# A two-layer graph network on one core: the edge check split over two engines, the mixing weights folded ahead of the branch, the MLP's start no longer tied to the degrees, bias additions and padding rows written elsewhere in the order

## The chip, the cores and the metric

The kernel runs on one core of one Trainium2 chip. The time is that of one execution on the device, in microseconds (us). The engines of the core are named as in the profile: PE (TensorE, matrix products; PEld is its weight load), DVE (VectorE), ACT (ScalarE), POOL (GpSimd) and SP (SyncE, which here only issues transfers). Each engine works through its own queue in order; semaphores hold an instruction until its inputs are there. Transfers are issued on SP's and ACT's queues, the indirect ones (gathers by index) on POOL's.

## The reference

The graph has 3125 nodes with 256 features and 50000 edges, sorted by their target. `xn` is the layer norm of `x`.

```python
# layer 0
xn = layernorm(x)
h = xn @ W                                   # gnn: messages
deg = segment_sum(1, dst);  dis = where(deg > 0, rsqrt(max(deg, 1)), 0)
gnn = segment_sum(h[src] * (dis[src] * dis[dst])[:, None], dst)
hm = layernorm(xn, ln1_g, ln1_b) @ Wx + bx   # mix: 8 heads of 32
q = softmax(heads(hm) @ Wq, -1);  k = softmax(heads(hm) @ Wk, over the nodes)
fx = merge(q @ (k.T @ (heads(hm) @ Wv))) @ Wo + bo + xn
mix = gelu(layernorm(fx, ln2_g, ln2_b) @ W1 + b1) @ W2 + b2 + fx
x = x + gnn + mix
# soft experts: all 8 experts for every node, weighted
z = layernorm(x);  w = softmax(z @ Wr + br)
x = x + sum_e w[:, e] * (relu(bn2(relu(bn1(z @ W1[e])) @ W2[e])) @ Wo[e] + bo[e])
# layer 1: attention over the edges, a hyperbolic mixer, a shared MLP
# and the two best of 8 experts for every node (routed by index)
```

## The kernel before

Nodes are tiled as T = 25 tiles of P = 125 nodes, in seven chunks of four tiles (the last has one). `X` holds the running sum, `XN` the current normalised input, both in SBUF for the whole run.

**Prologue.** The edge list may be used in blocks only if the edges of each tile lie within 128 × LE = 2176 entries of the sorted list. To check this the kernel loads `dst` and counts, for each of the 25 tiles, how many targets lie below its bound (L309 to L311, 25 passes of ACT over 125 × 400 values with a sum). A product with ones adds the partitions (L317), a chain of small DVE operations makes `lidx` (rows of the edge list to fetch) and `nbi` (the number of misfits), and a branch on `nbi` (L2142) selects the usual path, `in_order`, which this input takes. Beside it DVE normalises all 25 tiles (L346 to L372). The prologue's order on each engine is found by the framework's scheduler.

**Layer 0** (class `Layer0`). The body is a set of generators, and `Flow` writes their order out by hand: each `yield Op(engine, cost, after, take, give, lag)` states a planned cost, marks of other steps that must be planned before, and buffers taken and given back. `Flow.run` always emits next the step that can start first by the plan, and on a tie the stream of lower urgency. The plan fixes the order of instructions on each engine; in the run an instruction waits only for the data and buffers that it really uses.

- `first` (L663) loads the weights of the stage and folds the norm's gain into `wx` and `xb` (four groups of small products and DVE operations, L692 to L720).
- `listing` (L786) fetches the edge lists by 25 indirect gathers, turns the target columns (`dl`) by PE and writes them to DRAM (`dlT`). For each tile it then reads them back broadcast to all partitions (`db`, 544 KB each, two buffers), and a Sign pass on ACT with a sum (L823) counts; a product and a Newton root give `dis`.
- `mix_in` transposes a chunk (`tr_mix`) and projects it (`xm`, L855); `messages` makes `hU` (L868, scaled by ACT); `q_softmax`, `k_softmax` and `mix_out` form the attention; `kw` is the last product of the key side, and `at` (L971) gives `fx`, one mark for each tile.
- `table` (L979) scales `hU` by `dis` and splits it into three bf16 parts by turns of ACT and DVE; SP writes them to the table `hs3`.
- `bias` (L1043) adds `mix_b2` to `X` on POOL, one operation of 125 × 1024 for each chunk.
- `after_mixing` (L769) waits for all `fx`, all `hU` and `dis`, closes the pool of the mixing stage and loads the experts' weights (24 transfers of 256 KB); the mark `mixed` follows.
- `mlp_stream` (L561) is the MLP of a chunk: statistics and scaling on DVE, transposes, two activations into `hT`, eight products `hp` with a gelu each, and products `dn`. Its transposes wait for `mixed` by the plan.
- `edges` (L1004) needs `mixed` and all tables: for each tile, in three groups of up to six edge columns, POOL gathers message rows (`msg`, two buffers), DVE builds a 0/1 matrix `S` (three buffers), SP writes it out for layer 1 (`hot`), and PE sums.
- `after_mlp` waits for the MLPs and the tables; `soft_work` (L749) then writes the padding rows of the table `xs` (8,224 KB by one transfer; layer 1 uses `xs` for routing) and, behind it on the same queue, loads `f_bo`, `f_wr`, `w3` and `wc`.
- `soft_in`, `expert` and `soft_out` are the experts of a chunk, its second norm (mark `ch["d"]`) and the projections to `qtab` and `kvtab`; `ball` writes `ztab`. A chunk starts when its tiles have their edge sums.

**Layer 1** (from L1373) follows in a plan of its own.

The urgencies, in `mixing_flow` and `mlp_flow`, are −1 for `listing` and `k_softmax`, 0 for `mix_in` and `mix_out`, 1 to 3 for the others of the stage, 4 for `edges`, 5 for the MLP, 10 and more for the experts.

Of the kernel before, what the change touches and what calls it, by code (L numbers as in the profile page):

```python
# [7 lines left out]
F32 = mybir.dt.float32  # L8
# [3 lines left out]
OP = mybir.AluOpType  # L12
# [138 lines left out]
def kernel(ctx: ExitStack, tc: tile.TileContext, a: dict, out: bass.AP):  # L151
# [41 lines left out]
    check = ExitStack()  # L193
    edge = check.enter_context(tc.tile_pool(name="check", bufs=1))
# [4 lines left out]
    nc.scalar.dma_start(out=nxt, in_=a["dst"][1 : E + 1].rearrange("(p j) -> p j", j=EP))  # L199

# [27 lines left out]

    away = keep.tile([128, 128], F32, name="away")
# [4 lines left out]
    before = keep.tile([128, 128], F32, name="before")  # L234
    nc.vector.tensor_scalar(before, away, 0.0, None, op0=OP.is_lt)
# [18 lines left out]
    zeros = keep.tile([128, W], F32, name="zeros")  # L254
    nc.vector.memset(zeros, 0.0)
# [30 lines left out]
    def turned(dst_, src_, nt, name, nk=2, g=None, b=None):  # L286

        for k in range(nk):
# [6 lines left out]
            else:  # L295
# [6 lines left out]
    bound = edge.tile([P, T], F32, name="bound")  # L302
    nc.gpsimd.iota(bound, pattern=[[P, T]], base=P, channel_multiplier=0,
                   allow_small_or_imprecise_dtypes=True)
    nc.vector.tensor_scalar(bound, bound, -0.5, None, op0=OP.add)
# [3 lines left out]
    for b in range(T):  # L309
        nc.scalar.activation(sign, dstf, AF.Sign, bias=bound[:, b : b + 1], scale=-1.0,  # L310
                             accum_out=cnt[:, b : b + 1])  # L311
    nc.vector.tensor_tensor(below, dst, nxt, OP.is_gt)
    nc.vector.tensor_reduce(cnt[:, T:], below, AX.X, OP.add)
    with ExitStack() as st:
        psum(st, nm=1)
        pc = nm_tile([128, T + 1], "counts")
        nc.tensor.matmul(pc, allone[:P, :], cnt, start=True, stop=True)  # L317
        ends = edge.tile([128, T + 1], F32, name="ends")
        nc.vector.tensor_scalar(ends[:, :T], pc[:, :T], 0.5, E / 2.0, op0=OP.mult, op1=OP.add)
        nc.vector.tensor_copy(ends[:, T:], pc[:, T:])  # L320
# [21 lines left out]


# [3 lines left out]
    mva = check.enter_context(tc.tile_pool(name="norm", bufs=1)).tile([P, T, 2], F32, name="mva")  # L347
    ra = small.tile([P, T], F32, tag="ra", name="ra", bufs=1)
    rb = small.tile([P, T], F32, tag="rb", name="rb", bufs=1)
    for c0, c1 in ((0, 2), (2, 4), (4, 7)):  # L350
        for c in range(c0, c1):
            t0, nt = CHUNKS[c]
            for j in range(nt):
                st_ = small.tile([P, 6], F32, tag="st", name=f"st_a{c}_{j}")
                nc.vector.bn_stats(st_, X[c][:, j, :])
                nc.vector.bn_aggr(mva[:, t0 + j, :], st_)
        ts = slice(CHUNKS[c0][0], CHUNKS[c1 - 1][0] + CHUNKS[c1 - 1][1])
        var = mva[:, ts, 1]
        nc.vector.tensor_scalar(rb[:, ts], var, 1e-5, None, op0=OP.add)
        nc.scalar.activation(ra[:, ts], rb[:, ts], AF.Sqrt)  # L360
        nc.vector.reciprocal(ra[:, ts], ra[:, ts])
        nc.vector.reciprocal(rb[:, ts], rb[:, ts])
        nc.vector.tensor_tensor(rb[:, ts], rb[:, ts], var, OP.mult)
        nc.vector.tensor_scalar(rb[:, ts], rb[:, ts], 1e-5, None, op0=OP.add)
        nc.scalar.activation(irs[:, ts], rb[:, ts], AF.Sqrt)
        nc.vector.reciprocal(rb[:, ts], irs[:, ts])
        nc.vector.tensor_tensor(ra[:, ts], ra[:, ts], rb[:, ts], OP.mult)
        for c in range(c0, c1):
            t0, nt = CHUNKS[c]
            for j in range(nt):  # L370
                nc.vector.tensor_scalar(XN[c][:, j, :], X[c][:, j, :], mva[:, t0 + j, 0:1],
                                        ra[:, t0 + j : t0 + j + 1], op0=OP.subtract, op1=OP.mult)  # L372
# [15 lines left out]
    nc.sync.dma_start(out=qtab[N : N + 1, :], in_=zeros[:1, :C])  # L388


    def degrees():
        with tc.tile_pool(name="deg", bufs=1) as dp:
# [20 lines left out]
            HJ = EP // 2  # L413
            hot_b = dp.tile([P, P, HJ], BF16, name="hot_b")
            hot_a = dp.tile([P, T, HJ], BF16, name="hot_a")
            for g in range(2):
# [18 lines left out]
    def slow_load(pool):  # L435
# [3 lines left out]
        for name, pad in (("src", 0), ("dst", N)):  # L439
# [8 lines left out]
            )  # L448
        e["dstf"] = pool.tile([128, EJ], F32, name="all_dstf", bufs=1)
# [23 lines left out]
    def slow_edges0(e):  # L473
# [4 lines left out]
        with tc.tile_pool(name="e0", bufs=3) as ep:  # L478
            G = 4
            for g in range(EJ // G):  # L480
# [5 lines left out]
                nc.vector.tensor_tensor(sb, S, before[:, None, :].to_broadcast([128, G, 128]), OP.mult)  # L486
# [74 lines left out]
    def mlp_stream(c, inputs, name, pool_of, w1, w2, g, b, b1, done, start):  # L561
# [20 lines left out]
        mk = yield Op("PE", 0.48 * nt, [m, start], take=["mm", "mm", "mlp"])  # L582
# [49 lines left out]
    NQ = NH * 4  # L632
    WX = C + 1 + 2 * NQ
    Q0, K0 = C + 1, C + 1 + NQ

    class Layer0:
# [26 lines left out]
        def first(self):  # L663
# [3 lines left out]
            self.hUt = lp.tile([P, T, C], F32, name="hU")  # L667
            mp = self.mix = self.open("mix", side="right")
            self.wx = mp.tile([128, 2, WX], F32, name="wx")
            wxr = self.wxr = mp.tile([128, 2, C], F32, name="wxr")  # L670
            nc.sync.dma_start(out=wxr, in_=a["Wx"].rearrange("(k p) d -> p k d", p=128))
            wxT = mp.tile([128, 2, C], F32, name="wxT")
            nc.sync.dma_start(out=wxT, in_=a["WxT"].rearrange("(k p) d -> p k d", p=128))
            wqk = mp.tile([128, 2, 2 * NQ], F32, name="wqk")
            nc.sync.dma_start(out=wqk, in_=a["Wqk"].rearrange("(k p) d -> p k d", p=128))
# [1568 lines left out]
```

## Time and profile before

| what | value |
| --- | --- |
| median of 3 runs | 2831.29 us (2821.73 to 2831.99) |
| profiled execution, time | 2825.43 us |
| its span in the trace | 2823.6 us |
| mean granted clock of PE in it | 0.953 |
| PE busy | 2502.8 us, 89% |
| branch entered (first issue behind it) | 41.11 us |
| `dis` ready | 195.6 us |
| table written, first message gather | about 260 us |
| MLP's last product, then the padding's issue | about 424 us, 428.59 us |
| last message gather | about 858 us |
| experts of layer 0 end | about 1275 us |

The page gives the busy time of each engine, then the span in forty slices of 70.6 us, each digit the busy share in tenths. A row of the timeline reads: start, length, engine, line, operation, output and inputs, how many were merged, and in brackets the idle time before it and what ended it. Two things help: an idle engine that is not the bound costs nothing, and the row of a transfer on SP shows its issue, so that a long one means a queue that was full.

### The profile page before, as it was taken

What the parts mean: (1) busy time and instruction counts of PE and PEld (TensorE: products, weight loads), DVE (VectorE), ACT (ScalarE), POOL (GpSimd) and SP (SyncE); (2) the same over time, 40 slices, a digit from 0 to 9 for tenths busy, and PEclk for the clock granted to TensorE, in tenths of its full rate; (3) what the DMA queues carried; (4) which work ended last, traced back from release to release, by engine and by line L of the source; (5) the groups of instructions that cost most, each with busy time, mean ns of one, the idle gap of its engine ahead of it and who ended that gap; (6) DMA issues with size and microseconds to landing.
All of it is one profiled execution on the core that took longest, in us unless ns stands there. A gap on an engine that the chain in (4) does not pass through costs nothing. (4 is left out here: it accounts for less than half of the span.)

```text
span 2823.6 us, 32362 instructions
## 1 busy us (share of the span) xinstructions
PE 2502.8 (89%) x11409; PEld 1822.1 (65%) x11409; DVE 1404.1 (50%) x3527; ACT 963.8 (34%) x2020; POOL 1158.5 (41%) x1145
## 2 busy tenths in 40 slices
PE   3769994999999989996778988888888999999998
PEld 2436773666665645564556756666666668888885
DVE  5476112253453243445889888988886301111113
ACT  3465111222233333444334444444442222222221
POOL 3202774777771000002766655655522632222220
PEclk9869996999999999998889999999999999999999
DMA  4263668666661011106766665666630245555545
GB/s 109 97 201 108 174 177 242 176 190 197 177 199 50 1 33 55 41 25 223 226 199 197 213 196 168 193 188 207 193 110 1 64 162 195 196 196 188 196 147 141
DMA packets 187211, 427.02 MB, mean 151 GB/s; under 512 B 31644, under 2 KB 116765, under 8 KB 178846
## 3 DMA queue, kind: packets, MB, share of 16 engines
q0 software_dynamic: 80688, 281.78, 32.7%
q1 hardware_dynamic: 104650, 141.38, 16.0%
q10 hardware_dynamic: 1700, 1.69, 0.2%
q8 instruction: 92, 1.51, 0.2%
q14 instruction: 81, 0.66, 0.1%
HBM read 358.95 MB, written 65.74 MB: 150 GB/s over the span
## 5 line engine op out<-in xcount | busy, mean ns | idle before, releaser
L1431 POOL DMA_INDIRECT kvg<-kvtab,el x425 | 461.2, 1085 | 312.8 <-issue 105.8
L1010 POOL DMA_INDIRECT msg<-hs,el x425 | 423.2, 996 | 337.7 <-DMA hot<-S 175.2
L1119 ACT ACTIVATE fh<-fp,bnh,bns 128x500 f32<-128x500 f32 (+1 forms) x224 | 160.5, 723 | 357.8 <-PE fp L1115 357.6
L1508 PE MATMUL es<-kvg,S 128*125 128x264 f32 x850 | 226.4, 419 | 50.0 <-DVE kvg L1500 49.6
L1986 PE MATMUL rh<-xrT,rw 128*128 128x256 f32 x1024 | 237.2, 380 | 0.0
L1974 ACT ACTIVATE rhid<-rh,rw 128x256 f32<-128x256 f32 x256 | 121.5, 475 | 336.8 <-PE rh L1986 336.8
L2001 PE MATMUL ry<-rw,rhid 128*128 128x256 f32 x1024 | 231.5, 379 | 0.0
L1508 PEld LDWEIGHTS es<-kvg,S 128*125 128x125 f32 x850 | 166.9, 202 | 98.6 <-DVE kvg L1500 66.1
L1130 DVE SCALAR_TENSOR_TENSOR x<-fy,f_w,x 125x256 f32<-125x256 f32 x200 | 96.3, 482 | 264.7 <-PE fy L1127 263.8
L1033 PEld LDWEIGHTS <-S 128*125 128x125 bf16 x1275 | 155.1, 140 | 91.1 <-issue 80.0
L2001 PEld LDWEIGHTS ry<-rw,rhid 128*128 128x128 f32 x1024 | 194.6, 190 | 26.9 <-issue 0.5
L1127 PE MATMUL fy<-f_Wo,fh 128*125 128x256 f32 x800 | 206.6, 383 | 5.1 <-DVE x L1130 4.9
L1467 PE MATMUL qe<-q,ST 125*128 125x256 bf16 x1275 | 171.7, 276 | 43.5 <-DVE kvg L1471 37.5
L1986 PEld LDWEIGHTS rh<-xrT,rw 128*128 128x128 f32 x1024 | 189.4, 190 | 28.5 <-ACT rhid L1974 5.0
L2008 DVE TENSOR_TENSOR yr<-ry,rw 128x256 f32<-128x256 f32 x64 | 27.2, 425 | 357.5 <-PE ry L2001 357.5
L1033 PE MATMUL es<-msg,S 128*125 128x256 bf16 x1275 | 184.3, 278 | 22.2 <-DMA msg<-hs,el 20.5
L1115 PE MATMUL fp<-fh,f_W 128*128 128x500 f32 (+1 forms) x448 | 187.2, 546 | 0.3 <-ACT fh L1119 0.3
L1115 PE MATMUL fp<-xT_f,f_W 128*128 128x500 f32 (+1 forms) x448 | 185.2, 540 | 0.0
L1243 POOL TENSOR_TENSOR xn<-xn,row_bp 125x1024 f32<-125x1024 f32 (+1 forms) x7 | 13.8, 1978 | 416.9 <-PE tr_q L554 209.4
L1127 PEld LDWEIGHTS fy<-f_Wo,fh 128*125 128x125 f32 x800 | 143.4, 189 | 62.3 <-issue 37.8
L1467 PEld LDWEIGHTS <-ST 125*128 125x128 bf16 x1275 | 125.3, 99 | 79.2 <-issue 46.6
L1471 DVE TENSOR_TENSOR kvg<-qe,kvg 128x512 f32<-128x512 f32 (+1 forms) x225 | 142.8, 651 | 28.9 <-PE qe L1467 18.7
(420 smaller groups left out, 4235.0 us busy)
## 6 DMA issues: line engine op xcount, KB each, us to landing
db<-dlT SPq DMA_DIRECT2D x25, 544.0 KB
ST<-dlT SPq DMA_DIRECT2D x25, 544.0 KB
hot<-S SPq DMA_DIRECT2D x50, 187.5 KB
Sb<-hot SPq DMA_DIRECT2D x50, 187.5 KB
ztab<-z SPq DMA_DIRECT2D x18, 500.0 KB
z<-ztab SPq DMA_DIRECT2D x12, 750.0 KB
xs<-pad SPq DMA_DIRECT2D x1, 8224.0 KB
xr<-xs SPq DMA_DIRECT2D x32, 257.0 KB
```

Source lines behind the costliest of these rows:

```text
L1010: nc.gpsimd.indirect_dma_start(out=msg[:, i, :], out_offset=None, in_=hs3_rows, in_offset=bass.IndirectOffsetOnAxis(ap=el[:, b, g0 + i : g ...
L1033: nc.tensor.matmul(blk["po"], S[:, i, :], msg[:, i, r * C : (r + 1) * C], start=(g0 + i == 0 and r == 0), stop=(g0 + i == LE - 1 and r == 2))
L1115: nc.tensor.matmul(ps[q][:, :n], self.ws[e][i][:, k, q * 128 : (q + 1) * 128], h[:, k, :n], start=(k == 0), stop=(k == 1))
L1119: nc.scalar.activation(nxt[:, q, :n], ps[q][:, :n], AF.Relu, bias=self.sh[i][:, 2 * e + q : 2 * e + q + 1], scale=self.sc[i][:, 2 * e + q ...
L1127: nc.tensor.matmul(po, nxt[:, k, j * P : (j + 1) * P], self.ws[e][2][:, k, :], start=(k == 0), stop=(k == 1))
L1431: nc.gpsimd.indirect_dma_start(out=kvg[:, i, : 2 * C], out_offset=None, in_=kvtab, in_offset=bass.IndirectOffsetOnAxis(ap=el[:, b, g0 + i ...
L1467: nc.tensor.matmul(pq[i0][:, i, :], ST[:P, g0 + i0 + i, :], blk["q3"][:, r, :], start=(r == 0), stop=(r == 2))
L1471: nc.vector.tensor_tensor(kvg[:, i0 : i0 + k, :C], pq[i0][:, :k, :], kvg[:, i0 : i0 + k, :C], OP.mult)
L1508: nc.tensor.matmul(blk["pa"], S[:, i, :], kvg[:, i, C:], start=(g0 + i == 0), stop=(g0 + i == LE - 1))
L1974: nc.scalar.activation(hid[-1][:, q % 2, :], ps, AF.Gelu, bias=w1[:, 8 * C + q : 8 * C + q + 1])
L1986: nc.tensor.matmul(ps, w1[:, k * 4 * C + h * 128 : k * 4 * C + (h + 1) * 128], xrT[:, k, :], start=(k == 0), stop=(k == 1))
L2001: nc.tensor.matmul(po, hid[k // 2][:, k % 2, r * 128 : (r + 1) * 128], w2[:, k * C : (k + 1) * C], start=(k == 0), stop=(k == 7))
```

## The change

1. The edge check: the first 12 bounds are counted on ACT as before, the other 13 by DVE (compare and sum); the bounds are made at the very start. The prologue is now written in a fixed order instead of one found by the scheduler.
2. The loads of `Wx`, its transpose, `Wqk` and the biases, and the folding into `wx` and `xb`, stand in the prologue. Their loads are on ACT's queue, and the products that read them stand partly ahead of the counting product. The tiles live in the pool that stays open; layer 1 reuses their memory for `bd` and `b_res`.
3. Only chunks 0 and 1 are normalised in the prologue; the others are streams of the plan (`normal`), half of the scaling on ACT.
4. `listing` is split into streams (`turned_lists`, `degree`, `degrees`). The degrees' transfers are planned behind the 17th projection.
5. `after_mixing` does not wait for `dis`; the MLP does not wait for `mixed`, and its first two chunks have urgency −1. 21 of the 24 expert weights are loaded in `after_mixing`, three in `soft_work`.
6. `table` works on two tiles at a time, scales on ACT, and uses the `db` buffers; `XT` has five buffers.
7. `bias` is planned behind `kw`; the padding rows are written behind chunk 1's `ch["d"]`.

```diff
     check = ExitStack()
+    check.enter_context(tc.manual_schedule(engines=ENGINES))
...
+    bound = edge.tile([P, T], F32, name="bound")
+    nc.gpsimd.iota(bound, pattern=[[P, T]], base=P, channel_multiplier=0, ...)
+    nc.vector.tensor_scalar(bound, bound, -0.5, None, op0=OP.add)
...
+    nc.scalar.dma_start(out=wxr, in_=a["Wx"].rearrange("(k p) d -> p k d", p=128))
+    nc.scalar.dma_start(out=wxT, in_=a["WxT"].rearrange("(k p) d -> p k d", p=128))
+    nc.scalar.dma_start(out=wqk, in_=a["Wqk"].rearrange("(k p) d -> p k d", p=128))
+    nc.scalar.dma_start(out=bxt, in_=a["bxT"])
+    bx = row(edge, "bx", 128)
...
-    for b in range(T):
+    TA = 12
+    for b in range(TA):
         nc.scalar.activation(sign, dstf, AF.Sign, bias=bound[:, b : b + 1], scale=-1.0,
                              accum_out=cnt[:, b : b + 1])
+    for b in range(TA, T):
+        nc.vector.tensor_scalar(below, dstf, bound[:, b : b + 1], None, op0=OP.is_lt, op1=OP.add,
+                                accum_out=cnt[:, b : b + 1])
     nc.vector.tensor_tensor(below, dst, nxt, OP.is_gt)
     nc.vector.tensor_reduce(cnt[:, T:], below, AX.X, OP.add)
+    for k in range(2):
+        nc.vector.tensor_scalar(wx[:, k, :C], wxr[:, k, :], col("ln1_g", k), None, op0=OP.mult)
+    pb = nm_tile([128, C], "bxm")
...
+    pc = nm_tile([128, T + 1], "counts")
+    nc.tensor.matmul(pc, allone[:P, :], cnt, start=True, stop=True)
...
+    for _ in normal(0, 2, None):
+        pass
     check.close()
...
-    def mlp_stream(c, inputs, name, pool_of, w1, w2, g, b, b1, done, start):
+    def mlp_stream(c, inputs, name, pool_of, w1, w2, g, b, b1, done, start=None):
...
-        mk = yield Op("PE", 0.48 * nt, [m, start], take=["mm", "mm", "mlp"])
+        mk = yield Op("PE", 0.48 * nt, [m] + ([start] if start else []), take=["mm", "mm", "mlp"])
...
         def soft_work(self):
             fp = self.ffn = self.open("ffn")
-            pad = fp.tile([128, C + 1], F32, name="pad")
...
+            self.expert_weights(fp, NE - 1)
+
+        def padding(self, ch):
+            yield Op("POOL", 1.0, [ch["d"]])
+            pad = self.ffn.tile([128, C + 1], F32, name="pad")
+            nc.gpsimd.memset(pad[:, :C], 0.0)
+            nc.gpsimd.tensor_scalar(pad[:, C:], part, float(2 * N), None, op0=OP.add)
+            yield Op("SP", 0.2)
+            nc.sync.dma_start(out=xs.rearrange("(q p) d -> p q d", p=128), ...)
 
         def after_mixing(self):
-            m = yield Op("SP", 2.5, self.fx + self.hu + [self.dis_])
+            m = yield Op("SP", 2.5, self.fx + self.hu)
             self.close("mix")
-            self.soft_weights()
             if self.lists:
                 self.e0 = self.open("e0", side="right")
-            self.mlp_work()
+            self.soft_weights()
             self.mixed.set(m)
...
+        def degree(self, b):
+            m = yield Op("SP", 3.3, [self.rows_[b // 7], self.xm[16]], take=["db"], lag=1.5)
+            db = self.low.tile([128, 128 * LE], BF16, tag="db", name=f"db_{b}", bufs=2)
+            nc.sync.dma_start(out=db, ...)
+            m = yield Op("ACT", 2.25, [m], give=["db"])
+            nc.scalar.activation(db, db, AF.Sign, bias=half, accum_out=self.cnt[:, b : b + 1])
+            self.counted[b].set(m)
...
         def table(self, c):
-                m = yield Op("DVE", 0.4, [self.dis_, self.hu[t]])
-                nc.vector.tensor_scalar(h, h, dis[:, t : t + 1], None, op0=OP.mult)
+                    m = yield Op("ACT", 0.42, [self.dis_, self.hu[t]])
+                    nc.scalar.activation(h, h, AF.Copy, scale=dis[:, t : t + 1])
...
+                m = yield Op("ACT", 0.4 * k, [m], take=["db"])
+                db = self.low.tile([128, 128 * LE], BF16, tag="db", name=f"h3_{t}", bufs=2)
+                h3 = db[:P, : 6 * C].rearrange("p (t i d) -> p t i d", t=2, i=3)
...
         def bias(self, c):
-            yield Op("POOL", 2.0)
+            yield Op("POOL", 2.4, [self.bias_at])
...
         def mixing_flow(self, flow):
+            flow.add(0, normal(2, 4, self.normal))
+            flow.add(0, normal(4, 7, self.normal))
...
         def mlp_flow(self, flow):
-                flow.add(5, mlp_stream(c, self.fx, "m", lambda: self.work, self.w1, self.w2,
-                                       "ln2_g", "ln2_b", "mix_b1", self.mlp_[c], self.mixed))
+                flow.add(5 if c > 1 else -1, mlp_stream(c, self.fx, "m", lambda: self.work, self.w1, self.w2,
+                                       "ln2_g", "ln2_b", "mix_b1", self.mlp_[c]))
...
         def soft_flow(self, flow):
+                if c == 1:
+                    flow.add(10, self.padding(ch))
```

## The prediction

> **What bounds the kernel now.** I read the busy shares first, then the forty slices, then busy time by stretch, and only then the timeline and the waits of the stretches where TensorE (PE) falls short. First the page:
>
> ```profile
> PE 2502.8 (89%) x11409; PEld 1822.1 (65%) x11409; DVE 1404.1 (50%) x3527; ACT 963.8 (34%) x2020; POOL 1158.5 (41%) x1145
> ...
> PE   3769994999999989996778988888888999999998
> ...
> PEclk9869996999999999998889999999999999999999
> ```
>
> PE is busy 89% of the span: PE work is the bound, and time can be won only where PE idles or runs at a low granted clock. In the part that the change touches (slices 0 to 17) the weak slices are 0 to 2 (up to 212 us) and slice 6 (424 to 494 us). The same by stretch (columns: length, busy time and count of PE, weight loads, DVE, ACT, POOL, then granted clock, DMA share, GB/s):
>
> ```profile
> 0.00:41.30 41.30, 0.63 (x2) 0.50 (x2) 26.35 (x129) 20.85 (x58) 1.14 (x12) 1.00 0.42 90
> 41.30:54.40 13.10, 9.60 (x40) 8.82 (x40) 2.31 (x10) 2.31 (x4) 9.53 (x10) 1.00 0.90 275
> ...
> 73.00:89.00 16.00, 2.83 (x16) 2.03 (x14) 16.00 (x10) 0.00 (x0) 14.95 (x8) 0.66 0.01 2
> ...
> 149.50:206.00 56.50, 37.97 (x96) 22.03 (x96) 45.42 (x176) 33.75 (x49) 0.00 (x0) 0.59 0.65 205
> 206.00:262.00 56.00, 55.86 (x195) 36.31 (x196) 46.10 (x168) 36.76 (x89) 0.00 (x0) 0.95 0.32 96
> ...
> 428.00:472.00 44.00, 9.09 (x40) 6.82 (x40) 4.17 (x17) 2.34 (x3) 11.07 (x13) 0.54 1.05 288
> ...
> 858.00:1275.00 417.00, 406.53 (x1405) 242.88 (x1404) 161.68 (x497) 149.53 (x274) 18.75 (x9) 0.98 0.10 30
> ```
>
> Four holes: the prologue (41 us without PE); 73 to 89 (13 us idle); 149.5 to 206 (38 us busy at a clock of 0.59, so 22 us of full-speed work: 34 us lost); 428 to 472 (35 us idle). From 206 to 1275 PE is otherwise full, so what is saved in the holes shifts everything behind them. What ends each hole (timeline, start and length):
>
> ```profile
> 40.29 0.15 DVE L339 CAST nbi<-nbad 128x1 int32<-128x1 f32 x1
> ...
> 41.34 3.57 PE L843 MATMUL tr_mix<-ident,xn 125*128 125x125 f32 x16 [4.60 <-DVE wx L692]
> ...
> 54.53 2.45 PE L855 MATMUL xm<-wx,XT 128*125 128x321 f32 x4
> ...
> 73.09 15.30 DVE L803 TENSOR_SCALAR dl<-el 128x17 bf16<-128x17 int32 x7
> 73.45 14.51 POOL L1046 TENSOR_TENSOR x<-x,row_mix_b 125x1024 f32<-125x1024 f32 x7
> ...
> 206.14 16.23 PE L608 MATMUL hp_m<-hT_m,mw 128*128 128x500 f32 x32 [12.56 <-ACT hT_m L592]
> ...
> 428.59 0.37 SPq L754 DMA_DIRECT2D xs<-pad  x1
> 429.06 29.82 SPq L759 DMA_DIRECT2D f_bo<-in_f_bo  x1
> ```
>
> The branch waits for the edge check (nbi), the first projection for the weights folded behind the branch, DVE's dl for POOL's seven additions of mix_b2, and the MLP (hp_m) for the degrees. For the last hole, the waits between 425 and 475 us:
>
> ```profile
> PE rt L1066 <- DMA f_wr<-in_f_Wr: 25.9, 1, 25.9
> ...
> POOL msg L1010 <- PE es L1033: 32.2, 1, 32.2
> ```
>
> The 8,224 KB of padding fill SP's queue; f_bo and f_wr stand behind them, the router matmul waits 25.9 us for f_wr, and the gathers then wait for PE.
>
> **The change part by part.** Sums are against the profiled execution, 2825.4 us (span 2823.6), 5.9 us under the median of 2831.3.
>
> *Prologue, −11 us.* Removed: 25 Sign passes on ACT at 0.63 + 0.19, one each 0.75 us, from 15.9 to 36.1, because their bounds came late in DVE's order (15.65). Now 12 on ACT (9.0 us) beside 13 compare-and-sum passes on DVE, from dstf at 7.3 on. No row shows that form; the nearest are the 400-wide compare and the 400-wide sum, 0.57 us each, so 7.4 us; below, 0.5 each by the 256-wide scaling (0.33) stretched; above, 0.57 + 0.19 if the sum is read out apart (9.9). I take 0.57: done at about 17. The counting matmul, however, now stands behind products that read Wx. Five loads are added to ACT's queue (0.4 us of issue each, ahead of the first Sign at 7). There dst took 0.7 to 6.9 and nxt to 12, 5.1 us per 195 KB beside the loading of x; pv and Wx, 363 KB more, land near 21.5 (bounds: 15 if they get the 275 GB/s of 41 to 54 us, 28 if x leaves them less). Then 2.0 + 1.7 + 0.6 us of PE (the bxm, bxT and counts rows) and 3.5 of DVE (36.8 to 40.3): nbi at 29.5. List gathers, 42.1 before, begin near 30. DVE still folds (3.5 us) and normalises 8 tiles (4.5 statistics, 2.5 chain, 1.5 for the scaling shared with ACT) ahead of the branch, so the first transposes stay at 41.5, but the first projection follows at 43.5 instead of 54.5. Between the bounds: −5 to −16. The other 17 normalisations (17 × 0.8 + 5 = 19 us) go into the branch, on a DVE that was busy 12 of the 32 us from 41.3 to 73: hidden. If that cover is gone they cost up to 8 us, half of them.
>
> *The mix_b2 additions, 0 us.* They get a later place in the written order, but POOL's queue is the same: 25 list gathers, seven additions, then the message gathers. The mark for kw is a planning time and no data dependency; the additions read X and the bias row. So they run as soon as the lists end, now near 61 to 76, and DVE's next contended operation waits again. Price between −13 us (the stall gone) and +3 (DVE has more to do there); I take 0. The row: one dl operation took 14,306 ns, through all seven additions. The Trainium skill ("SBUF — State Buffer", section "Who interferes with whom") has the shared port pair locked for one whole instruction. By that alone DVE would be let in after one addition (2.3 us) and the sum would be about 11 us lower; the row contradicts it, and I keep the row.
>
> *MLP without the degrees, −22 us.* The start mark, and dis in after_mixing, go. Chunks 0 and 1 come first, at urgency −1. Before, kw was ready at 149.5 and the first hp ran at 206.1; fx of chunk 0 exists at 154. With mixing 11 us earlier, kw is at 138 and hp can run from about 150, between the attention products. Of the 34 us lost from 149.5 to 206 I take two thirds, because ACT has little room: 25 signs at 2.1 + 0.19 = 57 us within 88 us, and now MLP activations (6.9 us a chunk: 8 × 0.67 + 2 × 0.77) in the same order. Bounds: 0 (all lost to ACT) and −34.
>
> *Degrees and tables, 0 us.* Lists are 12 us earlier, the stall stays, each db block still takes 3.5 us (88 us for 25): dis at 180 instead of 195.6. The table's scaling moves from DVE to ACT (25 × 0.42 = 10.5 us), casts go in pairs through the two db buffers: about 50 us instead of 55.4 on SP, so message gathers start near 232 instead of 262. That is worth nothing by itself: PE is full from 206 on, and gathers end long before the experts do (858 against 1275). Cover: MLP, 184 us of PE, lasts past 300.
>
> *Expert weights, +3 us.* 21 of 24 loads of 256 KB no longer wait for dis; three move into soft_work. Behind them on SP may stand a few db loads (24 took 16.6 us of issue); on ACT a sign waits, and MLP activations behind it. I take 3 us for one short hold-up, 0 to 20.
>
> *Padding, −19 us.* Behind mlped, f_wr is now first in line: the 35 us go. The same 8,224 KB now start after chunk 1 of the experts. That was near 775 us (first kvtab write of the chunk 779.9), with message gathers alive until 858. POOL's two small operations (0.33 + 0.22) are nothing; but SP stands again for 30 us, and behind it stand hot, kvtab, qtab and ztab writes. DVE needs the first hot write back for its fourth S tile, some 27 us on at one group each 8 to 9 us, and the first qkv buffer for tile 2, some 22 us on (kvtab writes lie 7 to 9 us apart); the padding takes about 41 (428.6 to 469.5). DVE then stands 14 to 20 us and PE behind it, with experts to do until then. I take 16. Ends: 0 (all covered) and 35.
>
> *Layer 1's bd and b_res in kept tiles, the smaller constants:* one load each as before, nothing on the path.
>
> Sum: −11 − 22 + 3 − 19 = −49: 2776 against the profiled execution, 2782 as a median.
>
> **The rivals.**
> - *The padding is covered, or the additions no longer hold DVE* (another −11 to −29): experts of chunk 2 have no hot buffer in their way, which speaks for it; that PE's order is fixed and holds edge sums every 8 us speaks against. About 2762.
> - *ACT is the limit from 150 to 230:* MLP activations stand behind signs that wait for db, so PE gains 5 instead of 22 and the prologue 8. ACT busy 33.75 of 56.5 us speaks against, the 9.4 us that signs waited for db for it. 2825.4 − 8 − 5 + 3 − 16 = 2799, as a median 2805.
> - *The change does little:* the padding costs its 35 us again and the rest is half: 2831 − 10 = 2821.
> - *Slower: the degrees fall behind the weights.* The weights reuse memory of the mixing stage, and SP takes them in order. If they are issued with 15 db loads still to come, SP stands until the last attention product (about 175), 16 us of weights follow, then 15 × 3.5 = 52: dis near 250, tables to 305, chunk 0's edge sums at 305 + 68 × 1.26 = 391, while the MLP is done near 350. PE then idles about 70% of 41 us, and ACT has stood for some 20: together they eat the 49. The point of decision is dis at 250; at 280 the time is about 2850. Against it: in the trace the last message product's copy (192.1) lies behind the last sign, and after_mixing still waits for all of those.
>
> **How the numbers follow.** The forecast, 2782 (2768 to 2796), has 0.45; the better case 0.18; ACT's limit 0.18; little change 0.10; slower 0.09. Low end 2755, high end 2821: this leaves out the slower case and the tail of the better one. About 0.5%, 14 us, can be told from no change: faster (under 2817) 0.81, same 0.10, slower 0.09.
>
> **What would show it.** Right: nbi near 30, first projection near 43, hp_m before dis, no wait of rt for f_wr, and a dip of PE near 700 us under the padding. Wrong: dl waiting for nothing, hp_m only after the last sign, dis later than 200, or a hole in PE between the MLP and the first experts.

## The result, and the profile after

The changed kernel takes 2790.5 us (median; 2784.7 to 2797.0) against 2826.5 us for the kernel before in the same series. The ratio is 0.9877, with a 95% interval of 0.9838 to 0.9916. The profiled execution took 2788.9 us (span 2787.1) against 2825.4: 36.5 us less, where the prediction's sum had 49. The direction and the range were right, and most of the mechanism; two terms of the sum were not.

First the page of the changed kernel: busy times, and the forty slices (now of 69.7 us each) for PE and its granted clock.

```profile
PE 2491.7 (89%) x11409; PEld 1815.1 (65%) x11409; DVE 1397.5 (50%) x3493; ACT 967.2 (35%) x1995; POOL 1155.4 (41%) x1145
...
PE   3889999999599999996778888888898999999998
...
PEclk8989989999899999997899999999999999999999
```

The same 11,409 products took 11.1 us less (2502.8 to 2491.7, at a mean granted clock of 0.960 instead of 0.953), and PE was idle for 25.4 us less (span minus busy: 320.8 to 295.4). That is the whole gain. Slices 1 and 2 are fuller than before. The weak slice of before, number 6, is gone, and there is a new one, number 10, from 697 us on. By stretch (columns as in the prediction: length, then busy time and count of PE, weight loads, DVE, ACT, POOL, granted clock, DMA share, GB/s):

```profile
0.00:41.30 41.30, 13.60 (x54) 11.29 (x54) 28.15 (x119) 16.36 (x38) 12.55 (x24) 1.00 0.72 180
58.00:72.20 14.20, 0.69 (x7) 0.50 (x5) 14.20 (x2) 1.23 (x3) 14.18 (x8) 0.61 0.02 3
136.00:180.00 44.00, 34.19 (x92) 16.78 (x91) 30.79 (x123) 31.02 (x35) 0.00 (x0) 0.69 0.37 128
180.00:240.00 60.00, 59.93 (x223) 38.51 (x222) 41.45 (x122) 41.87 (x81) 0.00 (x0) 1.00 0.29 76
390.00:412.00 22.00, 15.56 (x92) 13.89 (x90) 8.61 (x29) 3.72 (x8) 15.91 (x17) 0.78 0.85 269
707.00:762.00 55.00, 24.07 (x103) 14.80 (x102) 16.77 (x57) 6.45 (x13) 22.05 (x23) 0.78 0.87 251
```

Of the four holes, the one of the prologue is partly filled: 13.6 us of PE in the first 41.3, where there was 0.63. The one under the additions is still there, with 13.5 of 14.2 us idle. The one ahead of the MLP is shorter, and PE is full from 180 us on instead of 206. The one under the padding has moved to 708 us and is nearly as large as it was: 30.9 us idle in the 55 us from the padding's issue, against 34.9 in the 55 us from 428 in the kernel before:

```profile
428.00:483.00 55.00, 20.09 (x82) 14.49 (x82) 8.96 (x35) 4.62 (x7) 17.56 (x20) 0.58 0.93 256
```

The rows of the timeline that answer to those of before:

```profile
21.89 0.62 PE L354 MATMUL counts<-cnt,allone 125*128 125x26 f32 x2 [0.54 <-ACT sign L321]
...
24.71 0.15 DVE L376 CAST nbi<-nbad 128x1 int32<-128x1 f32 x1
...
37.53 1.25 PE L896 MATMUL xm<-wxt,XT 128*125 128x321 f32 x4
...
57.88 14.28 DVE L931 TENSOR_TENSOR xmq<-xmq,qmx 125x128 f32<-125x128 f32 x1
58.13 14.62 POOL L1094 TENSOR_TENSOR x<-x,row_mix_b 125x1024 f32<-125x1024 f32 x7
...
164.34 6.59 PE L681 MATMUL hp_m<-hT_m,mw 128*128 128x500 f32 x8
...
707.99 0.37 SPq L803 DMA_DIRECT2D xs<-pad  x1
708.46 33.02 SPq L1068 DMA_DIRECT2D hot<-S  x1
741.57 1.06 SPq L210 DMA_DIRECT2D kvtab<-qkv  x2
```

The edge check's verdict is there at 24.7 us (40.3 before), the first projection at 37.5 (54.5). A DVE operation is again held, for 14.28 us, while the additions run. The MLP starts at 164 (206), and `dis` is first used at 181 (before it was ready at 195.6). The padding's issue is followed by an `hot` write that SP needs 33 us to issue. Last, the waits that start between 705 and 770 us (total, how often, longest):

```profile
ACT q L1219 <- DMA qtab<-q: 35.9, 1, 35.9
DVE qkv L1222 <- ACT q L1219: 27.6, 2, 27.1
POOL msg L1058 <- PE es L1081: 27.4, 2, 27.1
...
PE z L1274 <- ACT xT_hy L631: 25.6, 1, 25.6
```

ACT cannot write the next `q` because the single `q3` buffer waits for its transfer to `qtab`, which stands behind the padding in SP's queue. DVE waits for ACT, PE waits for the transposed rows that ACT owes it, and the gathers wait for PE.

### The profile page after: what moved, and what is told of

The parts are those of the page before. It is cut to its first block, busy times and chain, and to the rows that moved or that the text cites. A ratio compares the mean times of both kernels' runs of the same rounds, so it can differ in the third digit from the quotient of the medians.

```text
span 2787.1 us, 32246 instructions
## 1 busy us (share of the span) xinstructions
PE 2491.7 (89%) x11409; PEld 1815.1 (65%) x11409; DVE 1397.5 (50%) x3493; ACT 967.2 (35%) x1995; POOL 1155.4 (41%) x1145
## 5 line engine op out<-in xcount | busy, mean ns | idle before, releaser
L1534 PE MATMUL qe<-q,ST 125*128 125x256 bf16 x1275 | 171.5, 275 | 46.7 <-DVE kvg L1538 41.3
L1538 DVE TENSOR_TENSOR kvg<-qe,kvg 128x512 f32<-128x512 f32 (+1 forms) x225 | 143.0, 652 | 29.0 <-PE qe L1534 17.8
```

Of the source, the lines that this page charges most:

```text
L1534: nc.tensor.matmul(pq[i0][:, i, :], ST[:P, g0 + i0 + i, :], blk["q3"][:, r, :], start=(r == 0), stop=(r == 2))
L1538: nc.vector.tensor_tensor(kvg[:, i0 : i0 + k, :C], pq[i0][:, :k, :], kvg[:, i0 : i0 + k, :C], OP.mult)
```

## The experiments

They ran on three other chips, where both kernels are 5 to 6% slower: the kernel before has medians of 2966, 2987 and 2984 us there. Times are therefore set only against kernels of the same chip; what their traces show of this stands in the last section. Where two medians of one chip are subtracted, the bound behind the difference is about 95%, from the scatter of the single runs.

### The changed kernel again

It was run on two of the three chips, as the base for the others.

> The changed kernel itself, on the chip and against the same runs of the kernel before as the three that follow, so that each can be set against it. Expected: the ratio measured first, 0.988 (0.984 to 0.992). On a chip where both kernels are slower by about 5%, the same 36 us would be 0.988; if the gain scaled with the time the ratio would not change either, so a ratio outside 0.984 to 0.992 would say that part of the gain depends on the chip.

> The changed kernel once more, only to have it on the same chip and against the same runs of the kernel before as the three that follow. Two chips so far gave 0.988 and 0.991; expected between 0.984 and 0.994.

Measured: 2957.5 us, ratio 0.9908 (0.9875 to 0.9941), and 2950.4 us, ratio 0.9881 (0.9856 to 0.9905). Within the intervals, the gain is the same share on each chip.

### The padding, moved alone in the kernel before

First to the place that the change gives it (behind chunk 1 of the experts), then behind the last message gather of layer 0:

```diff
-            pad = fp.tile([128, C + 1], F32, name="pad")     # in soft_work, ahead of f_bo and f_wr
...
+        def padding(self, ch):
+            yield Op("POOL", 1.0, [ch["d"]])                 # second kernel: [self.e0_[T - 1]]
...
+                if c == 1:
+                    flow.add(10, self.padding(ch))
```

> The kernel before with one part of the change alone: the padding behind chunk 1's second norm. Prediction: 35 us of PE hole become 16, so 19 us less than before, ratio about 0.993. Rival from the changed kernel's trace (a hole of 30 us at the new place, and 6 us left at the old): no measurable change, ratio 0.998 to 1.001.

> The kernel before with one step of the change alone, put elsewhere: the padding rows behind the last message gather of layer 0 instead of ahead of the router's weights; nothing else. Behind chunk 1 of the experts, as the change has it, this step alone was worth nothing (0.999). Theory: the 35 us that PE stood in the kernel before go, and behind the last gather nothing is held, so 28 to 35 us, a ratio near 0.989. Rival: that the hole is the same wherever the padding stands, a ratio of 0.997 or more.

Measured: 0.9991 (0.9968 to 1.0013) at the change's place, and 0.9911 (0.9882 to 0.9940) behind the last gather, which is 27 us of that chip's 2984 (33 us by the medians). The stretch from the padding's issue on, in the first kernel, then in the second:

```profile
807.00:862.00 55.00, 25.11 (x93) 16.30 (x94) 11.29 (x22) 7.27 (x15) 19.16 (x22) 0.72 0.88 252
```

```profile
909.00:964.00 55.00, 55.00 (x198) 32.76 (x197) 17.49 (x56) 16.36 (x23) 0.35 (x2) 1.00 0.72 177
```

At the change's place 29.9 of 55 us of PE are lost; behind the last gather, none. So this step of the change, as it was made, is worth nothing that can be told from the scatter (the interval reaches to 9 us). It removes a hole of 35 us and makes one of 30. Put some 100 us later, the same step alone gives nearly as much as the whole change on that chip: three quarters by the ratios (0.9911 against 0.9881), almost all by the medians (2951.4 against 2950.4 us).

### The padding in the changed kernel: last, in pieces, and with a second q3

```diff
-            yield Op("POOL", 1.0, [ch["d"]])
+            yield Op("POOL", 1.0, [self.e0_[T - 1] if self.lists else ch["d"]])
```

> The changed kernel, but the padding transfer is planned behind the last edge sum of layer 0 instead of behind chunk 1's second norm; all else is as it was. Theory (the padding still costs a hole in PE, only at another place: from 708 to 757 us PE is busy 18.7 of 49 us): in the stretch after the last message gather SP has nothing to write until chunk 2's projections, so the hole goes and nothing takes its place: 30 us less than the changed kernel, about 2760, ratio to the kernel before about 0.977. Rival (the hole only shifts: chunk 2's writes to kvtab and qtab then wait as chunk 1's did, and PE stands for them): 2785 to 2795, ratio about 0.987.

Measured: 2906.8 us, ratio 0.9803 (0.9777 to 0.9829). The stretch from the padding's issue on:

```profile
907.00:962.00 55.00, 55.00 (x213) 33.88 (x212) 28.12 (x100) 19.47 (x31) 0.93 (x3) 1.00 0.70 177
```

No hole is left. The theory's ratio lies just below the interval, the rival's well above it.

```diff
-            yield Op("SP", 0.2)
-            nc.sync.dma_start(out=xs.rearrange("(q p) d -> p q d", p=128), ...)
+            xv = xs.rearrange("(q p) d -> p q d", p=128)
+            nq = NT * ROUTE // 128 // 16
+            for i in range(16):
+                yield Op("SP", 2.5)
+                nc.sync.dma_start(out=xv[:, i * nq : (i + 1) * nq, :], ...)
```

> The changed kernel with the padding at the same place in 16 pieces of 514 KB, each a step of 2.5 us for SP's order, so that hot, kvtab and qtab writes can stand between them. Theory: the hole is made by writes that stand behind 8 MB in one queue and not by the bandwidth that the padding takes; with pieces each write waits for at most a few pieces, the 30 us hole shrinks to 10 us or less and the time falls by 18 to 28 us. Rival: the padding takes the engines of the DMA as a whole (1.05 of their share while it ran in the kernel before), and gathers and writes are as late as in one piece; the time stays within 6 us of the changed kernel.

Measured: 2933.1 us, ratio 0.9844 (0.9807 to 0.9880), 17 us (plus or minus 14) below the changed kernel on the same chip. From the padding's issue on, twice 55 us in the changed kernel on this chip, then the same in the one with pieces, and SP's queue in the latter:

```profile
795.00:850.00 55.00, 25.37 (x107) 15.80 (x106) 16.54 (x60) 7.05 (x15) 20.81 (x22) 0.75 0.88 247
850.00:905.00 55.00, 52.73 (x228) 33.95 (x227) 18.67 (x35) 12.08 (x21) 41.10 (x40) 0.97 0.68 202
```

```profile
785.00:840.00 55.00, 48.22 (x218) 30.85 (x216) 27.27 (x74) 8.77 (x15) 40.13 (x40) 1.00 1.05 305
840.00:895.00 55.00, 45.35 (x200) 29.45 (x198) 15.66 (x29) 13.75 (x24) 30.57 (x32) 0.91 0.66 193
```

```profile
785.26 3.21 SPq L806 DMA_DIRECT2D xs<-pad  x4
788.57 1.29 SPq L1071 DMA_DIRECT2D hot<-S  x1
789.91 4.00 SPq L806 DMA_DIRECT2D xs<-pad  x3
794.01 6.20 SPq L1071 DMA_DIRECT2D hot<-S  x1
```

The hole shrinks from 29.6 to 6.8 us while the DMA engines move more than before (305 GB/s against 247). So the hole is not made by the bandwidth that the padding takes. It is made by small writes that stand behind 8 MB in one queue. Some of the gain goes again at once: in the next 55 us PE idles 9.7 us instead of 2.3. Over both stretches 15.5 us are won, which fits the 17 measured better than the 23 of the first stretch does. By the times alone the rival (within 6 us) is not excluded; the trace decides.

```diff
-                q3 = fp.tile([P, 3, C], BF16, tag="q3", name=f"q3_{t0 + j}")
+                q3 = fp.tile([P, 3, C], BF16, tag="q3", name=f"q3_{t0 + j}", bufs=2)
...
-                        xh=2, xT=3, f_w=2, wT=1, ex=2, fh=3, qkv=2, q3=1)
+                        xh=2, xT=3, f_w=2, wT=1, ex=2, fh=3, qkv=2, q3=2)
```

> The changed kernel with a second buffer for the three bf16 parts of q (one buffer before), nothing else. Theory, from the waits: while the padding fills SP's queue, the first thing that stops is ACT, on the write of q out of the one buffer; with two buffers the next to stop are the hot writes and the second tile of q, some 8 to 14 us later, so the hole in PE shrinks from 30 us to 16 to 22 and the time falls by 8 to 14 us. Rival: the hole is the queue's, whichever buffer is first; the edge sums stand for the hot write as long in any case, the hole stays at 27 to 30 us and the time within 4 us of the changed kernel.

Measured: 2944.0 us, ratio 0.9847 (0.9808 to 0.9886), 13.5 us (plus or minus 12) below the changed kernel. The stretch in the changed kernel on this chip, then in this one, and this one's waits that start between 780 and 840 us:

```profile
794.00:849.00 55.00, 27.12 (x114) 16.19 (x113) 18.78 (x65) 6.64 (x14) 22.37 (x24) 0.78 0.85 254
787.00:842.00 55.00, 31.03 (x139) 19.78 (x138) 24.12 (x84) 10.13 (x20) 25.33 (x27) 0.81 0.92 277
```

```profile
ACT z L1281 <- DVE stats L1277: 25.0, 1, 25.0
...
PE qkv L1203 <- DVE qkv L1206: 21.5, 1, 21.5
DVE qkv L1206 <- DMA kvtab<-qkv: 19.9, 1, 19.9
```

The hole is 24.0 us instead of 27.9 on this chip: smaller, but not by the 8 to 14 us that the theory wanted. With a second `q3`, what holds the work is the `qkv` buffer's write to `kvtab`, in the same queue, which the theory did not name. The hole lies between the theory (16 to 22) and the rival (27 to 30), and shows that a second buffer of one kind handed most of the wait to the next. The time fell by as much as the theory said and by more than the hole did; where the rest comes from is not settled (the first gather of layer 1 comes 8 us earlier in the profiles, 1344.5 against 1352.8, and the interval reaches down to 2 us).

### The additions, after the keys' exponential

The row that the additions read is loaded only behind the exponential of the keys, so they cannot run beside the projections:

```diff
-            self.mb2 = row(lp, "mix_b2")
+            self.mb2 = lp.tile([128, C], F32, name="row_mix_b2")
...
             nc.scalar.activation(kn, kn, AF.Exp)
+            nc.scalar.dma_start(out=self.mb2, in_=...)
```

> The changed kernel, but the row mix_b2 is loaded by ACT's queue behind the exponential of the key softmax, so that POOL's seven additions have to wait for it (near 105 us) and meet DVE while it waits for PE. Theory (the later place in the written order did nothing, the additions run when the list gathers end and hold DVE for 14 us, and with it PE and the degrees): the DVE operation of 14.28 us at 58 us shrinks to 0.3, the rows dlT are written 14 us earlier, dis comes 12 to 15 us earlier, and the time falls by 10 to 14 us against the changed kernel, to about 2778. Rival (the stall is covered, since PE's idle time there returns in the wait for ACT or the db transfers): the DVE operation shrinks likewise, but the time stays within 4 us of 2790. Second rival: DVE is held at the new place as long as it was at the old: also about 2790, with a long DVE operation near 110 us.

> The changed kernel with two edits at once: the padding rows behind the last message gather of layer 0, and the bias row of the additions loaded only behind the exponential of the keys, so that the additions run beside the projections' end. Theory: the two holes are separate and the gains add: -26 to -30 us for the hole under the padding and -7 to -14 for the hole under the additions, 33 to 44 us below the changed kernel, a ratio near 0.974 against before. Rival: the hole under the additions is given back behind it (the message gathers did not start earlier in the changed kernel either), so that only the padding's 26 to 30 us come, a ratio near 0.978.

Measured: 2925.1 us, ratio 0.9873 (0.9840 to 0.9906) for the additions alone, on the chip where the padding behind the last gather gave 2906.8. With both edits, on another chip: 2919.2 us, ratio 0.9764 (0.9723 to 0.9805), 38 us (plus or minus 13) below the changed kernel there.

On these chips the additions of the changed kernel do not run in one row, as they did in the first measurement. ACT stops from 45.5 to 61.8 us (last section), so chunks are normalised later, and POOL may add to a chunk of `X` only when its normalisation has read it. The changed kernel on the second chip:

```profile
57.77 4.65 POOL L1094 TENSOR_TENSOR x<-x,row_mix_b 125x1024 f32<-125x1024 f32 x2
65.22 3.10 DVE L432 TENSOR_SCALAR xn<-x,mva,vb 125x256 f32<-125x256 f32 x3
65.76 2.40 POOL L1094 TENSOR_TENSOR x<-x,row_mix_b 125x1024 f32<-125x1024 f32 x1 [3.35 <-DVE xn L432]
68.86 1.98 DVE L840 TENSOR_SCALAR dl<-el 128x17 bf16<-128x17 int32 x1
75.24 4.88 POOL L1094 TENSOR_TENSOR x<-x,row_mix_b 125x1024 f32<-125x1024 f32 x2 [4.44 <-DVE xn L432]
75.42 2.37 DVE L840 TENSOR_SCALAR dl<-el 128x17 bf16<-128x17 int32 x1
77.70 2.57 DVE L432 TENSOR_SCALAR xn<-x,mva,vb 125x256 f32<-125x256 f32 x1
```

DVE is held four times for about 2 us each, some 8 us in all, and not once for 14: alone, three of these `xn` take 1.05 us, one takes 0.38 and a `dl` 0.17. With the row loaded late the additions are one row again (first of the two kernels):

```profile
121.10 14.60 POOL L1097 TENSOR_TENSOR x<-x,row_mix_b 125x1024 f32<-125x1024 f32 x7 [62.88 <-DMA row_mix_b<-in_rv]
```

They take 14.6 us as before, but DVE runs nothing from 117.0 to 139.8 us: it waits for PE there, so nobody is held. `dis` is first used at 183.7 us in the kernel with both edits, against 192.5 in the changed kernel on that chip: 8.8 us earlier (on the first chip 5.8, against the kernel with the padding last) and not the 12 to 15 expected, since the long hold was not there to be removed. If the two gains add, the sum is 38 us by the second chip and the difference 18 by the first, so 28 us belong to the padding and 10 to the additions, each plus or minus some 9. That they add is taken for granted in this; the interval of the kernel with both edits reaches to 0.9805, so the times alone do not exclude the rival's 0.978. The 10 us fit the 8 us of short holds. What the single hold of 14.28 us costs on the chip of the first measurement is not shown by any run. The kernel with both edits has the lowest ratio of all: the change gave 0.9908 on its chip, the change with these two edits 0.9764.

### The MLP bound to the degrees again

```diff
-            m = yield Op("SP", 2.5, self.fx + self.hu)
+            m = yield Op("SP", 2.5, self.fx + self.hu + [self.dis_])
...
-                flow.add(5 if c > 1 else -1, mlp_stream(...))
+                flow.add(5, mlp_stream(..., self.mixed))
```

> The changed kernel with one part undone: the MLP's transposes wait by the plan for the mark behind the mixing stage again, that mark for the degrees, and all chunks of the MLP have urgency 5. Theory of the prediction (untying the MLP is worth 22 us): about 2812, with the first hp product after the degrees and a PE hole of some 20 us more between 136 and 200 us. Rival (ACT, full of signs, had let little of the MLP through before the degrees; the gain lay in the earlier start): 2793 to 2798.

> The changed kernel with the MLP bound to the degrees again (its start mark, its urgency and the wait of the weights for the degrees as before), now beside the changed kernel on the same chip. The trace of the first run of this edit has PE busy only 11 of the 40 us from 180 to 220, against 40 of 40 with the MLP free, and the experts of layer 0 some 37 us later than in a run with the MLP free. The prediction: the freed MLP is worth 22 us, so this kernel is 20 to 24 us slower than the changed one (ratio to it near 1.0075). By the trace: 27 to 34 us slower (near 1.010). Rival: the work that was pulled forward leaves the same gap later; less than 10 us slower (below 1.0035).

Measured: 0.9950 (0.9930 to 0.9970) on the first of the three chips, and 2969.4 us, 0.9948 (0.9930 to 0.9966), on the third, where the changed kernel has 2950.4: 19 us slower (plus or minus 9). From 140 to 220 us, the changed kernel on that chip, then the one with the MLP bound:

```profile
140.00:180.00 40.00, 30.36 (x90) 15.52 (x90) 23.14 (x89) 29.50 (x33) 0.00 (x0) 0.65 0.49 162
180.00:220.00 40.00, 39.86 (x140) 24.01 (x139) 28.54 (x95) 28.65 (x52) 0.00 (x0) 0.96 0.16 45
```

```profile
140.00:180.00 40.00, 36.45 (x110) 18.97 (x109) 22.54 (x72) 25.43 (x29) 0.00 (x0) 0.68 0.46 149
180.00:220.00 40.00, 11.18 (x24) 5.54 (x24) 35.11 (x147) 24.15 (x41) 0.00 (x0) 0.51 0.62 194
```

Bound, PE works 6 us more from 140 to 180 (on attention products that the changed kernel does later) and 29 less from 180 to 220, at half the clock: 22.6 us net. The measured 19 agrees with that and with the prediction's 22. These two runs also say what the rest of the change is worth: with the MLP bound, all else stays, and the kernel is still some 15 us (9 to 21) below the kernel before on both chips. My reading of the first trace, 27 to 34 us, was too high, since it set two kernels of which one also had late additions.

### The edge check on ACT alone

```diff
-    TA = 12
+    TA = 25
```

> The changed kernel with all 25 passes of the edge check on ACT again, the rest of the prologue as changed. Theory: the 13 passes that DVE took are 0.75 us each on ACT, so the counting matmul, the branch and everything behind it come 9 to 10 us later, and the time rises by 8 to 10 us over the changed kernel. The prediction's own working puts the shared check at 3 to 5 us only, since it held the products that read Wx (landing near 21.5 us) for the later limit. Rival: the gain of the shared check is hidden behind the first normalisations and the additions; the time stays within 3 us.

Measured: 2961.4 us, ratio 0.9907 (0.9877 to 0.9937), 4 us (plus or minus 9) above the changed kernel. The first product that reads `Wx`, the counting product and the first transposes:

```profile
12.83 2.05 PE L347 MATMUL bxm<-wxr,b_in 128*128 128x256 f32 x4 [12.83 <-DMA wxr<-in_Wx]
...
31.42 0.63 PE L354 MATMUL counts<-cnt,allone 125*128 125x26 f32 x2 [15.04 <-ACT sign L321]
...
43.83 3.68 PE L883 MATMUL tr_mix<-ident,xn 125*128 125x125 f32 x16 [7.03 <-DVE va L426]
```

The last two come 9.7 us later than in the changed kernel on that chip (21.65 and 34.11), and the first MLP product 9.4 us later (185.4 against 176.0). In time neither 9 to 10 us nor nothing is excluded. That the check shared by two engines moves the prologue by 9.7 us is shown; what of it reaches the end is not settled.

## Why the prediction was right, and where it was off

- *Prologue, −11 us: right in kind, more in size.* The verdict came at 24.7 us instead of the 29.5 forecast, the first projection at 37.5 instead of 43.5, which is 17 us earlier than before. The step that failed was the landing of `Wx`, put at 21.5 us with bounds of 15 and 28. The first product that reads it ran at 17.8, and it waited there for DVE, which stood behind its passes of the check. In the run with the check on ACT alone, on another chip, it waits for `Wx` itself and runs at 12.8, below the lower bound. The limit was the other one: ACT's twelve passes began at 12.8 and not at 7, behind the loads that ACT issues (the last of them at 11.2) and a 1.28 us load of the table for its function, and the counting product waited for the last pass at 21.9. DVE's compare-and-sum took 0.67 us from one pass to the next, a little above the 0.57 taken. The cover for the normalisations that moved behind the branch was not whole: PE stood 4.5 us ahead of 46.1 us, before transposes of tiles that DVE and ACT were still normalising (the forecast had 0, and up to 8 without cover).
- *The additions, 0 us: right where it was measured.* They ran at 58.1, three microseconds ahead of the stretch forecast, and one DVE operation took 14.28 us. It ended at 72.16, when the last and smallest of the seven had begun (71.9), so it was held through the six large ones; the same holds for the `dl` row of before, of which the prediction says all seven (held from 73.09 to 87.40, the seventh began at 87.24). Again this is not the one instruction of the Trainium skill ("SBUF — State Buffer", section "Who interferes with whom"); by that rule DVE would have been let in after about 2.3 us, an estimate from the length of one addition. On the chips of the experiments the holds are of about that length (1.98 and 2.37 us for a `dl`), as the rule has it; why six in a row kept DVE out on the other chip is open. Moving the additions to where DVE has nothing to do brought some 10 us (plus or minus 9) on the chips of the experiments, where the holds were short.
- *MLP without the degrees, −22 us: right.* Bound again it costs 19 us (plus or minus 9). The start, forecast near 150, was 164.3, because the normalised rows of the MLP came later, but PE was full from 180 us on.
- *Degrees and tables, 0 us: right, for `dis`* (forecast 180, used at 181), in part by luck: lists 12 us earlier, as the prediction had them, would put it at 183.6, and they came 15.6 us earlier; *wrong for the gathers:* forecast near 232, the first one went at 258.6, as before. Between the MLP's products the order left the last attention products until 236, and with them the weights that reuse their memory and the end of the table. The prediction had called this worth nothing as long as PE is full, and it was full.
- *Expert weights, +3 us: not measured alone.* The hole between the MLP and the first experts exists, but is small: 6.4 us idle from 390 to 412, where edge sums wait for message gathers. The router no longer waits for `f_wr`.
- *Padding, −19 us: the term that was mis-sized.* The forecast had a second hole of 16 us; it is 30.9, so the step brought 4 us in the trace, and nothing clear of the scatter by the run that makes it alone (0.9991). The bound of 35 had been given; the value taken between the bounds was wrong. It counted on 22 to 27 us in which PE would still have work, until the first `hot` or `qkv` buffer ran out. In the trace the buffer that ran out was `q3`, of which there is one. The run with two of them shows that this was not the whole of it: the wait for `kvtab`, which the prediction did name, then holds for 19.9 us, and the hole is still 24. The cover was too small even for the buffers that were counted.

The sum with what the runs showed: the prologue some −15 (the 14.7 us by which `dis` came earlier), MLP −19, padding −4, which is −38 against −36.5. That they agree so closely proves little, since the MLP's term carries 9 us and comes from another chip. The terms of the MLP and of the padding are each shown by a run that changes them alone. The rest, the prologue above all, is shown as a whole by the runs with the MLP bound, some 15 us, because the padding brings next to nothing there; how it divides among the edge check, the folding and the new order is not shown. That the time still lay within the forecast's band of 2768 to 2796 is in part luck: the prologue gave more than was forecast and made up for some of what the padding did not give.

Of the rivals, that with the padding covered was wrong at its centre, and so were ACT as the limit (PE was full from 180 on, not from 206) and the degrees behind the weights (`dis` was not late). The rival of little change was right that the padding costs its hole again, and wrong that the rest is halved.

## What to carry to other kernels

A large transfer that nobody waits for still has a price: it is paid by every small transfer behind it in the same queue, so its place should be where that queue has nothing urgent (here, after the last gather: no hole at all), or it should be cut into pieces that let others between. When such a step is moved, list all buffers whose release goes through that queue, with their numbers, and let the one with the fewest decide; the one buffer that was added here handed most of the wait to the next. And a hold of one engine by another (here of DVE by POOL's additions) can be shortened by moving the holder to where the held engine waits for something else.

## What the runs showed of the hardware

On the three chips of the experiments, engines stand still at times for which the trace has no releaser in the program. Such waits carry the word `remote`. Over the groups of waits that the profile lists (down to some 5 us), they come to 189 to 293 us in the twelve profiles of these chips, and to 0 us in the profiles of both kernels on the chip of the first measurement. One of them comes some 20 us behind the branch. ACT in the changed kernel there, whose branch is decided at 24.5 us, then in the kernel with the check on ACT alone, decided at 34.2:

```profile
44.92 0.58 ACT L890 COPY XT<-tr_mix 128x500 f32<-128x500 f32 x1 [5.81 <-remote]
61.83 0.47 ACT L913 ACTIVATE hU<-h,irs 125x256 f32<-125x256 f32 x1 [16.33 <-remote]
```

```profile
53.81 0.58 ACT L890 COPY XT<-tr_mix 128x500 f32<-128x500 f32 x1 [4.41 <-issue]
71.39 0.47 ACT L913 ACTIVATE hU<-h,irs 125x256 f32<-125x256 f32 x1 [17.01 <-remote]
```

The stop moves with the branch, by 9.6 us, so it is tied to the instructions behind it and not to the clock on the wall. The instruction queues' packets point the same way: in the changed kernel five of them are in the first 70 us on the chip without stops, four of these between 44 and 56, and on a chip with stops there are two, none between 30 and 62. (Only weakly: the kernel before has three in its first 70 us on the chip without stops, none between 44 and 56.) That these chips receive instructions later is an inference from this; no run here tests it. For the comparison it means that the same edit can be worth less where a stop changes the hole that it closes, as with the additions, whose long hold is not there on these chips.
